# Two experts' layers whose results are folded into the layer that follows them, and their first product a block ahead

## The chip, the core and the metric

The program runs on one core of one Trainium2 chip. The metric is the device time of one execution in microseconds (us); three executions of the kernel before took 2326.70, 2327.89 and 2333.26 us, median 2327.89. The engines are TensorE (PE, with its weight loads PEld), VectorE (DVE), ScalarE (ACT), GpSimd (POOL) and SyncE (SP, which here only issues DMAs). Each works through its own queue of instructions in order and waits for the others by semaphores.

## The reference, cut to what matters

x is [4, 1024, 128] in f32: 4096 tokens of width 128. The program computes these layers one after the other, each with a layer norm ahead of it and a residual behind:

```python
x = x + moe(layernorm(x))        # 8 experts, top 2, capacity, hidden 512
x = x + mamba(layernorm(x))      # d_inner 256, 16 states, conv of 4
x = x + moe(layernorm(x))        # the same weights again
x = x + 0.5 * soft(layernorm(x)) # 64 experts x 32 slots: x -> slots -> experts -> x
x = x + gla(layernorm(x))        # gated linear attention
x = x + 0.5 * soft(layernorm(x))
```

For the mixture of experts the part that matters is its end: every token has two slots (first and second choice), each expert's output for a slot is stored, and

```python
gathered = out[idx_k, loc_c]                       # [tokens, 2, 128]
y = einsum('tk,tkd->td', gates_k * valid, gathered)
```

so a token's new x is x + gate0 * row0 + gate1 * row1. After that, each token is normed by itself (mean and variance over its 128 values).

## The kernel before, in words

x stays in SBUF the whole time as 32 tiles of 128 tokens x 128 values; the code counts tiles (j, g) and treats four as a group, so there are eight groups. Each layer norm has three small arrays of one or two values a tile: mv (mean and variance), rstd and nmr (minus mean times rstd). `ln_group` (L137) fills them for one group: four pairs of bn_stats and bn_aggr on DVE (L121, L122), eps added on DVE (L123), a power of minus one half on POOL (L130), nmr on DVE (L133). `ln_apply` (L142) then norms one tile with one activation on ACT (L143).

**Experts.** `moe_layer` (L148) routes the tokens (transposed tiles xT, L242, and stores of the normed rows to DRAM, xn_d, on ACT's DMA queue), then runs the experts over 16 blocks of four slot tiles of 128 slots. For a block, POOL gathers the four tiles' rows by indirect DMA (L346), PE turns them (L364) and DVE copies them out (dT, L366), PE makes the hidden layer in four products ph (L374) which ACT takes out with relu (hT, L378), PE makes the output po (L388), DVE adds the bias (eo, L393), and POOL scatters the four tiles by indirect DMA to y_d in DRAM (L352), to the place of their token and choice. The loop (L399 to L418) writes hidden(blk), then gathers three blocks ahead alternating with scatters of the block before, then turn(blk + 1), then output(blk). It stands in a hand-ordered region: every compute engine's queue keeps the order in which the code is written, and only SP's queue is placed by the scheduler.

**Combine.** When all blocks are scattered, the eight groups are brought back (L421 to L438): for a group, two loads of y (both choices) on SP (L425), four activations on ACT that multiply the first choice by its gate (L427), four scalar_tensor_tensors on DVE that multiply the second choice by its gate and add x (L431), one add on DVE that writes x (L435), and then `after(j)`, the `ln_group` of the next layer's norm.

**Mamba.** `mamba_layer` (L441) cuts the sequence into four halves (2 sequences x 2). Each half has a `prologue` (L490), a generator that yields after each small step: norm four tiles (xn), turn them (pt) and copy (xT, L502), the convolution and the input products pu (L521), activations, the projection, the store of B and C rows to DRAM (bc_d), and the softplus chain of ACT and DVE that ends in delta and du (L577 to L583). The first half's prologue runs alone ahead of the main loop (L706), the others are spread into the loop. The main loop has 64 units; per unit DVE scans and POOL multiplies (L620, L638, L654).

**Between.** `soft_weights` norms the slot vectors phi (phiT) and makes a bias row that is stored to DRAM (pb_d, L789) and read back into phiT's last row (L790). In front of the soft layer a second phi (phiM) is copied from it (L1580), a row of minus ones (mone) is written over its last row by a DMA (L1583), and the branch on a flag is taken.

**Soft layer.** `soft_bounded` (L813) has a first phase of 64 steps k (half a tile's logits each): PE makes the logits l (L870), DVE their row minimum (nmh, L874), ACT the exponential ex (L879), DVE the sums over 32 slots and their reciprocal (sm, L886, L887), POOL the product dm (L891), PE adds it into px (L902). All is written in one loop (L1053) whose order is kept on each engine. Before it the first four tiles are normed, turned and copied to xT (L861), which POOL first presets with ones (L836); smod (L807, L810) is a small constant. The norm of the next four tiles runs in the steps themselves. The second phase (clogits, cexpo, cweigh, mix, finish) uses phiM, and its large tiles L come from the pool lp.

Of the kernel before, what the change touches and what calls it, by code (L numbers as in the profile page):

```python
# [8 lines left out]
F32 = mybir.dt.float32  # L9
# [8 lines left out]
P = 128  # L18
# [50 lines left out]
def macaron_kernel(ctx: ExitStack, tc: tile.TileContext, a: dict, out: bass.AP):  # L69
# [48 lines left out]
    def ln_stats(ln, j0, n=4):  # L118
        for j in range(j0, j0 + n):
            st = small.tile([P, 6], F32, name="st", bufs=4)  # L120
            nc.vector.bn_stats(st, x[:, j, :])  # L121
            nc.vector.bn_aggr(ln[0][:, j, :], st)  # L122
        nc.vector.tensor_scalar(  # L123
            ln[1][:, j0 : j0 + n], ln[0][:, j0 : j0 + n, 1], EPS, None, ALU.add
        )

    def ln_root(ln, j0, n=4):
        mv, rstd, nmr = ln
        js = slice(j0, j0 + n)
        nc.gpsimd.tensor_tensor(  # L130
            rstd[:, js], rstd[:, js], half_t.to_broadcast([P, n]), ALU.pow
        )
        nc.vector.scalar_tensor_tensor(  # L133
            nmr[:, js], mv[:, js, 0], -1.0, rstd[:, js], ALU.mult, ALU.mult
        )

# [11 lines left out]
    def moe_layer(w1, w2, b2, tag, ln, after):  # L148

        xn_d = dram.tile([T, D], F32, name=f"xn_d{tag}")  # L150
        with ExitStack() as s:
# [3 lines left out]
            gate = rp.tile([P, K, NT], F32, name="gate")  # L155
# [178 lines left out]
            with ExitStack() as s1:  # L334
                gp = s1.enter_context(tc.tile_pool(name=f"gath{tag}", bufs=16))
                wk = s1.enter_context(tc.tile_pool(name=f"ework{tag}", bufs=2))
                yp = s1.enter_context(tc.tile_pool(name=f"ey{tag}", bufs=3))
                ps = s1.enter_context(tc.tile_pool(name=f"eps{tag}", bufs=2, space=PSUM))
                psh = s1.enter_context(tc.tile_pool(name=f"epsh{tag}", bufs=3, space=PSUM))
# [59 lines left out]
                AHEAD = 3  # L399
                with tc.manual_schedule(engines=ENGINES):  # L400
                    for c in range(AHEAD * 4):
                        gather(c)
                    turn(0)
                    for blk in range(NBLK + 1):
                        if blk < NBLK:
                            hidden(blk)
# [8 lines left out]
                        if blk + 1 < NBLK:  # L415
                            turn(blk + 1)
# [3 lines left out]

                y_v = y2_d[: K * T, :].rearrange("(k j p) d -> p k j d", k=K, p=P)  # L421
                for j in range(0, NT, 4):
                    y = yp.tile([P, K, 4, D], F32, name="y")
                    for k in range(K):
                        nc.sync.dma_start(out=y[:, k, :, :], in_=y_v[:, k, j : j + 4, :])  # L425
                    for i in range(4):
                        nc.scalar.activation(  # L427
                            y[:, 0, i, :], y[:, 0, i, :], AF.Copy,
                            scale=gate[:, 0, j + i : j + i + 1],
                        )  # L430
                        nc.vector.scalar_tensor_tensor(  # L431
                            y[:, 1, i, :], y[:, 1, i, :], gate[:, 1, j + i : j + i + 1],
                            x[:, j + i, :], ALU.mult, ALU.add,
                        )
                    nc.vector.tensor_tensor(  # L435
                        x[:, j : j + 4, :], y[:, 0, :, :], y[:, 1, :, :], ALU.add
                    )
                    after(j)  # L438


    def mamba_layer(ln, ln_next):  # L441
# [3 lines left out]
        with ExitStack() as s:  # L445
# [258 lines left out]
            with tc.manual_schedule(engines=ENGINES):  # L704

                for _ in prologue(*halves[0], rs[0], psa, "dA"):  # L706
                    pass
# [105 lines left out]
    def soft_bounded(phiN, phiM, pbc, ew, eb, tag, ln, after=None, last=False):  # L813
# [11 lines left out]
        with ExitStack() as s:  # L825
# [4 lines left out]
            lp = s.enter_context(tc.tile_pool(name=f"slp{tag}", bufs=15))  # L830
# [218 lines left out]
            with tc.manual_schedule(engines=ENGINES):  # L1049
                for i in range(4):  # L1050
                    norm(i)
                turn(0)
                take(0)  # L1053
                for k in range(NK + CS * NB + XL + 3):
                    if k < NK:
# [487 lines left out]
    def moe(tag, ln, after):  # L1543
# [120 lines left out]
```

## Time and profile before

| | us |
|---|---|
| median of three executions | 2327.89 |
| the profiled execution | 2379.35 |
| its span, first to last instruction | 2377.5 |
| experts of the first layer, 76 to 269 | PE busy 148.0, POOL 126.8 |
| its combine, 269 to 304 | PE 4.9, DVE 26.4 |
| Mamba's first half, 304 to 345 | PE 17.2, ACT 19.2, DVE 9.1 |
| Mamba's loop, 345 to 881 | |
| route of the second experts' layer, 881 to 954 | |
| its experts, 954 to 1146 | |
| its combine, 1146 to 1188 | PE 2.2, DVE 26.9 |
| soft layer, first phase, 1188 to 1410 | PE 216.5, DVE 165.5, ACT 83.1, POOL 114.7 |
| soft layer, second phase, 1410 to 1682 | |
| gated linear attention, 1682 to 1878 | |
| second soft layer, 1878 to 2377 | |

A row of the profile gives a start in us, a duration, the engine, the line of the kernel, the operation, what it writes and reads (partitions x elements), how many instructions were joined to the row, and in square brackets how long the engine stood idle before it and what ended that. Times of the stages are read off the trace at the first instruction that belongs to a stage; stages overlap a little on single engines. All durations come from the one profiled execution. The granted clock of TensorE was 0.908 of full over the span, 0.50 in the second combine and 0.99 in the first phase of the first soft layer.

### The profile page before, as it was taken

How to read it: one execution, taken by the hardware profiler on the slowest of the kernel's cores; microseconds unless marked ns; L12 is line 12 of the kernel's file. 1: busy time of each engine (PE TensorE's matmuls, PEld its weight loads, DVE VectorE, ACT ScalarE, POOL GpSimd, SP SyncE). 2: the span in 40 equal slices, each digit the busy share in tenths (PEclk: the TensorE clock that was granted, in tenths of full speed). 3: DMA queues.
4: the chain of work that ended last, by engine and by line, in shares of the span. 5: the costliest groups of instructions: out<-in, count | busy, mean ns of one | idle time of the engine just before them, and what ended most of it. 6: DMA issues, size and time to landing. Idle time of an engine off the chain costs nothing. (4 is left out here: it accounts for less than half of the span.)

```text
span 2377.5 us, 17972 instructions
## 1 busy us (share of the span) xinstructions
PE 1946.3 (82%) x5889; PEld 908.7 (38%) x5889; DVE 1406.0 (59%) x1947; ACT 925.7 (39%) x1453; POOL 1399.4 (59%) x896
## 2 busy tenths in 40 slices
PE   4677548888888864777299998999888799989998
PEld 3444312333333324445144444444232344434443
DVE  4311438888888965111477764666688677764444
ACT  3222346565555523122233334333344233333331
POOL 1666428888888871666345556665344355556663
PEclk9999869999989885799699999999888699999999
DMA  6111322333232333111200000000000000000000
GB/s 239 34 44 46 91 99 94 111 98 103 94 110 94 110 127 111 43 47 42 83 1 0 0 1 1 1 1 0 6 0 1 1 0 0 1 1 5 9 10 15
DMA packets 63677, 111.23 MB, mean 47 GB/s; under 512 B 7999, under 2 KB 41423, under 8 KB 58581
## 3 DMA queue, kind: packets, MB, share of 16 engines
q1 hardware_dynamic: 45062, 81.37, 10.4%
q0 software_dynamic: 8192, 16.79, 2.5%
q10 hardware_dynamic: 10322, 11.85, 1.5%
q8 instruction: 48, 0.79, 0.1%
q14 instruction: 53, 0.43, 0.1%
HBM read 90.53 MB, written 19.44 MB: 46 GB/s over the span
## 5 line engine op out<-in xcount | busy, mean ns | idle before, releaser
L891 POOL TENSOR_TENSOR dm<-ex,sm 128x1024 f32<-128x1024 f32 x128 | 244.6, 1912 | 219.3 <-DVE sm L887 125.5
L654 POOL TENSOR_TENSOR hc<-hst,Cs 128x1024 f32<-128x1024 f32 x128 | 290.1, 2277 | 70.9 <-DVE hst L638 66.5
L669 PE MATMUL py<-hc,ident 128*128 128x512 f32 x512 | 279.6, 679 | 39.4 <-POOL hc L654 39.3
L999 POOL TENSOR_TENSOR acc<-acc,L 128x1024 f32<-128x1024 f32 x96 | 225.8, 2352 | 114.5 <-ACT L L991 113.9
L991 ACT ACTIVATE L<-pl,pbc 128x512 f32<-128x512 f32 x256 | 161.9, 683 | 282.6 <-PE pl L981 278.2
L870 PE MATMUL l<-phiT,xT 128*128 128x512 f32 x512 | 247.1, 607 | 15.2 <-ACT xT L861 8.7
L879 ACT ACTIVATE ex<-l,nmh 128x1024 f32<-128x1024 f32 x128 | 142.7, 1115 | 286.4 <-DVE nmh L874 284.2
L981 PE MATMUL pl<-xT,phiM 128*128 128x512 f32 x512 | 242.8, 598 | 0.0
L1025 PE MATMUL py<-L,yt 128*128 128x512 f32 x512 | 238.4, 593 | 4.4 <-DVE L L1015 4.4
L902 PE MATMUL px<-dm,xn 128*128 128x512 f32 x512 | 240.8, 593 | 0.9 <-POOL dm L891 0.9
L874 DVE TENSOR_REDUCE nmh<-l 128x1 f32<-128x1024 f32 x128 | 156.5, 1222 | 108.8 <-PE l L870 108.8
L628 ACT ACTIVATE dA<-delta,A 128x512 f32<-128x512 f32 x256 | 179.2, 722 | 93.0 <-DVE hst L638 89.9
L374 PE MATMUL ph<-dT,w 128*128 128x512 f32 x256 | 145.5, 682 | 60.8 <-ACT hT L378 43.5
L620 POOL TENSOR_TENSOR dBu<-du,Bs 128x1024 f32<-128x1024 f32 x80 | 172.7, 2159 | 37.9 <-ACT dA L628 37.9
L378 ACT ACTIVATE hT<-ph,cols 128x512 f32<-128x512 f32 x128 | 84.6, 686 | 283.4 <-PE ph L374 176.9
L352 POOL DMA_INDIRECT y_d<-eo,dest x128 | 125.8, 983 | 91.4 <-DVE eo L393 60.8
L669 PEld LDWEIGHTS py<-hc,ident 128*128 128x128 f32 x512 | 97.9, 205 | 199.0 <-issue 121.8
L638 DVE TENSOR_TENSOR_SCAN hst<-dA,carry,dBu 128x512 f32<-128x512 f32 x128 | 154.1, 1258 | 5.6 <-POOL dBu L620 5.6
L886 DVE TENSOR_REDUCE sm<-ex 128x32 f32<-128x1024 f32 x128 | 154.6, 1208 | 0.0
L870 PEld LDWEIGHTS l<-phiT,xT 128*128 128x128 f32 x512 | 97.4, 193 | 146.6 <-issue 115.9
L638 DVE TENSOR_TENSOR_SCAN hst<-dA,dBu 128x512 f32<-128x512 f32 x128 | 146.5, 1199 | 7.6 <-POOL dBu L620 7.5
L1015 DVE TENSOR_TENSOR L<-L,rd 128x1024 f32<-128x1024 f32 x128 | 147.0, 1210 | 0.1
(248 smaller groups left out, 2866.3 us busy)
## 6 DMA issues: line engine op xcount, KB each, us to landing
Cs<-bc_d SPq DMA_DIRECT2D x32, 1024.0 KB, 4.7
Bs<-bc_d SPq DMA_DIRECT2D x80, 256.0 KB, 3.3
w<-in_w SPq DMA_DIRECT2D x4, 2048.0 KB
y<-y_d SPq DMA_DIRECT2D x32, 256.0 KB, 3.5
y_d<-zero SPq DMA_DIRECT2D x1, 4096.0 KB
ew<-in_ew ACTq DMA_DIRECT2D x1, 4096.0 KB
x<-in_x SPq DMA_DIRECT2D x8, 256.0 KB, 8.5
xn_da<-xn ACTq DMA_DIRECT2D x8, 256.0 KB, 14.7
```

Source lines behind the costliest of these rows:

```text
L620: eng.tensor_tensor(dBu, r["du"], r.pop(("B", n)).unsqueeze(2).to_broadcast([P, HB, NC]), ALU.mult,)
L628: nc.scalar.activation(dA, r["delta"][:, :, c], AF.Exp, scale=A[:, c * DS + n : c * DS + n + 1],)
L638: nc.vector.tensor_tensor_scan(hst[:, :, c], r.pop(("dA", n, c)), dBu[:, :, c], 0.0 if h == 0 else carry[b][:, c, n : n + 1], ALU.mult, AL ...
L654: nc.gpsimd.tensor_tensor(hc, r.pop(("h", n)), Cs.unsqueeze(2).to_broadcast([P, HB, NC]), ALU.mult)
L669: nc.tensor.matmul(r["py"][:, c, :], ident, hc[:, :, c], start=False, stop=(n == DS - 1))
L870: nc.tensor.matmul(l[:, q * 512 : (q + 1) * 512], xT[:, j * P : (j + 1) * P], phiN[:, o : o + 512], start=True, stop=True,)
L891: nc.gpsimd.tensor_tensor(dms[k], exs.pop(k), sms.pop(k).unsqueeze(2).to_broadcast([P, NG, PS]), ALU.mult,)
L902: nc.tensor.matmul(px[hf * 2 + q], xns[j // 4][:, j % 4, :], dmf[:, q * 512 : (q + 1) * 512], start=(j == 0), stop=(j == NT - 1),)
L981: nc.tensor.matmul(pl[:, i, :], phiM[:, (2 * c + i) * P : (2 * c + i + 1) * P], xT[:, t * TB : (t + 1) * TB], start=True, stop=True,)
L991: nc.scalar.activation(L[:, i, :], pl[:, i, :], AF.Exp, bias=pbc[:, 2 * c + i : 2 * c + i + 1], scale=-1.0,)
L999: nc.gpsimd.tensor_tensor(accs[t], accs[t], L, ALU.add)
L1025: nc.tensor.matmul(pys[t], yt[:, 2 * c + i, :], L[:, i, :], start=(c + i == 0), stop=(c == CS - 1 and i == 1),)
```

## The change

- `moe_layer` ends with the last scatter. The combine becomes a function of its own, which returns `bring(j)` (the two loads of a group) and `pieces(j)`, a generator that does a group in eight pieces: four activations and two scalar_tensor_tensors; the other two; the add; two pairs of norm sums; two pairs and eps; POOL's power; the load of a later group; nmr. The gates move to tiles that live as long as the program.
- Mamba brings four groups, runs all pieces of group 0, and then runs three pieces after each yield of the first half's prologue. What is left runs behind it.
- The soft layer, inside the branch, brings two groups, runs group 0, norms and turns the first block, runs group 1, and then runs one piece ahead of each step k of its loop: groups 2 to 7 in steps 0 to 47. Only the first soft layer does this.
- The copy phiM, mone and its DMA are written ahead of the second experts' layer instead of inside the branch.
- The experts: hidden(blk + 1) and turn(blk + 2) are written where hidden(blk) and turn(blk + 1) were, with turn(1) and hidden(0) ahead of the loop, four blocks gathered ahead for three, 20 gather buffers for 16, three work buffers for two, four PSUM buffers of ph for three.
- The pool lp has 14 buffers for 15.

```diff
@@ -115,24 +115,37 @@
             const.tile([P, NT], F32, name=f"nmr{tag}"),
         )
-    def ln_stats(ln, j0, n=4):
+    def ln_sums(ln, j0, n=4):
         for j in range(j0, j0 + n):
             st = small.tile([P, 6], F32, name="st", bufs=4)
             nc.vector.bn_stats(st, x[:, j, :])
             nc.vector.bn_aggr(ln[0][:, j, :], st)
+    def ln_eps(ln, j0, n=4):
         nc.vector.tensor_scalar(
             ln[1][:, j0 : j0 + n], ln[0][:, j0 : j0 + n, 1], EPS, None, ALU.add
         )
-    def ln_root(ln, j0, n=4):
...
+    def ln_pow(ln, j0, n=4):
+        js = slice(j0, j0 + n)
+        nc.gpsimd.tensor_tensor(
+            ln[1][:, js], ln[1][:, js], half_t.to_broadcast([P, n]), ALU.pow
+        )
+    def ln_minus(ln, j0, n=4):
         mv, rstd, nmr = ln
         js = slice(j0, j0 + n)
-        nc.gpsimd.tensor_tensor(
-            rstd[:, js], rstd[:, js], half_t.to_broadcast([P, n]), ALU.pow
-        )
         nc.vector.scalar_tensor_tensor(
             nmr[:, js], mv[:, js, 0], -1.0, rstd[:, js], ALU.mult, ALU.mult
         )
+    def ln_root(ln, j0, n=4):
+        ln_pow(ln, j0, n)
+        ln_minus(ln, j0, n)
     def ln_group(ln, j0):
         ln_stats(ln, j0)
@@ -145,14 +158,13 @@
         )
-    def moe_layer(w1, w2, b2, tag, ln, after):
+    def moe_layer(w1, w2, b2, tag, ln, gate):
         xn_d = dram.tile([T, D], F32, name=f"xn_d{tag}")
         with ExitStack() as s:
             rp = s.enter_context(tc.tile_pool(name=f"route{tag}", bufs=1))
             src = rp.tile([P, NSB], I32, name="src")
             dest = rp.tile([P, NSB], I32, name="dest")
-            gate = rp.tile([P, K, NT], F32, name="gate")
             with ExitStack() as s1:
                 tp = s1.enter_context(tc.tile_pool(name=f"rtmp{tag}", bufs=1))
@@ -332,11 +344,10 @@
             with ExitStack() as s1:
-                gp = s1.enter_context(tc.tile_pool(name=f"gath{tag}", bufs=16))
-                wk = s1.enter_context(tc.tile_pool(name=f"ework{tag}", bufs=2))
-                yp = s1.enter_context(tc.tile_pool(name=f"ey{tag}", bufs=3))
+                gp = s1.enter_context(tc.tile_pool(name=f"gath{tag}", bufs=20))
+                wk = s1.enter_context(tc.tile_pool(name=f"ework{tag}", bufs=3))
                 ps = s1.enter_context(tc.tile_pool(name=f"eps{tag}", bufs=2, space=PSUM))
-                psh = s1.enter_context(tc.tile_pool(name=f"epsh{tag}", bufs=3, space=PSUM))
+                psh = s1.enter_context(tc.tile_pool(name=f"epsh{tag}", bufs=4, space=PSUM))
                 NBLK = NSB // 4
                 gs, dTs, hTs, eos = {}, {}, {}, {}
                 spacer = wk.tile([P, 1], F32, name="spacer")
@@ -396,14 +407,18 @@
-                AHEAD = 3
+                AHEAD = 4
                 with tc.manual_schedule(engines=ENGINES):
                     for c in range(AHEAD * 4):
                         gather(c)
                     turn(0)
+                    turn(1)
+                    hidden(0)
                     for blk in range(NBLK + 1):
-                        if blk < NBLK:
-                            hidden(blk)
+                        if blk + 2 < NBLK:
+                            turn(blk + 2)
+                        if blk + 1 < NBLK:
+                            hidden(blk + 1)
                         for i in range(4):
                             c = (blk + AHEAD) * 4 + i
                             if c < NSB:
@@ -412,33 +427,66 @@
                                 nc.gpsimd.memset(spacer, 0.0)
                             if blk > 0:
                                 scatter((blk - 1) * 4 + i)
-                        if blk + 1 < NBLK:
-                            turn(blk + 1)
                         if blk < NBLK:
                             output(blk)
-                y_v = y2_d[: K * T, :].rearrange("(k j p) d -> p k j d", k=K, p=P)
-                for j in range(0, NT, 4):
-                    y = yp.tile([P, K, 4, D], F32, name="y")
-                    for k in range(K):
-                        nc.sync.dma_start(out=y[:, k, :, :], in_=y_v[:, k, j : j + 4, :])
-                    for i in range(4):
-                        nc.scalar.activation(
-                            y[:, 0, i, :], y[:, 0, i, :], AF.Copy,
-                            scale=gate[:, 0, j + i : j + i + 1],
-                        )
-                        nc.vector.scalar_tensor_tensor(
-                            y[:, 1, i, :], y[:, 1, i, :], gate[:, 1, j + i : j + i + 1],
-                            x[:, j + i, :], ALU.mult, ALU.add,
-                        )
-                    nc.vector.tensor_tensor(
-                        x[:, j : j + 4, :], y[:, 0, :, :], y[:, 1, :, :], ALU.add
-                    )
-                    after(j)
-    def mamba_layer(ln, ln_next):
+    def combine(yp, gate, ln, n=2):
+        y_v = y2_d[: K * T, :].rearrange("(k j p) d -> p k j d", k=K, p=P)
+        ys = {}
+        def bring(j):
+            if j < NT:
+                y = ys[j] = yp.tile([P, K, 4, D], F32, name="y")
+                for k in range(K):
+                    nc.sync.dma_start(out=y[:, k, :, :], in_=y_v[:, k, j : j + 4, :])
+        def second(j, i):
+            nc.vector.scalar_tensor_tensor(
+                ys[j][:, 1, i, :], ys[j][:, 1, i, :], gate[:, 1, j + i : j + i + 1],
+                x[:, j + i, :], ALU.mult, ALU.add,
+            )
+        def pieces(j):
+            y = ys[j]
+            for i in range(4):
+                nc.scalar.activation(
+                    y[:, 0, i, :], y[:, 0, i, :], AF.Copy,
+                    scale=gate[:, 0, j + i : j + i + 1],
+                )
+            second(j, 0)
+            second(j, 1)
+            yield
+            second(j, 2)
+            second(j, 3)
+            yield
+            nc.vector.tensor_tensor(
+                x[:, j : j + 4, :], y[:, 0, :, :], y[:, 1, :, :], ALU.add
+            )
+            yield
+            ln_sums(ln, j, 2)
+            yield
+            ln_sums(ln, j + 2, 2)
+            ln_eps(ln, j)
+            yield
+            ln_pow(ln, j)
+            yield
+            del ys[j]
+            bring(j + 4 * n)
+            yield
+            ln_minus(ln, j)
+            yield
+        return bring, pieces
+    def run(pieces):
+        for _ in pieces:
+            pass
+    def mamba_layer(ln, ln_next, first):
         HB = 512
         NJ = HB // P
         bc_d = dram.tile([B, 2, 2, DS, HB], F32, name="bc_d")
@@ -702,9 +750,17 @@
                     f(rs[units[k][0]], units[k][1])
             with tc.manual_schedule(engines=ENGINES):
+                bring, pieces = first
+                for j in range(0, 16, 4):
+                    bring(j)
+                run(pieces(0))
+                others = (_ for j in range(4, NT, 4) for _ in pieces(j))
                 for _ in prologue(*halves[0], rs[0], psa, "dA"):
-                    pass
+                    for _ in range(3):
+                        next(others, None)
+                run(others)
                 for k in range(3):
                     at(fetch, k)
                 at(feed, 0)
@@ -827,7 +883,7 @@
             xnp = s.enter_context(tc.tile_pool(name=f"sxn{tag}", bufs=3))
             ep = s.enter_context(tc.tile_pool(name=f"sep{tag}", bufs=3))
             dp = s.enter_context(tc.tile_pool(name=f"sdp{tag}", bufs=4))
-            lp = s.enter_context(tc.tile_pool(name=f"slp{tag}", bufs=15))
+            lp = s.enter_context(tc.tile_pool(name=f"slp{tag}", bufs=14))
             wk = s.enter_context(tc.tile_pool(name=f"swk{tag}", bufs=4))
             psl = s.enter_context(tc.tile_pool(name=f"spl{tag}", bufs=2, space=PSUM))
             psm = s.enter_context(tc.tile_pool(name=f"spm{tag}", bufs=4, space=PSUM))
@@ -1047,11 +1103,21 @@
             SEAM = 3
             WL, XL = 10, 12
             with tc.manual_schedule(engines=ENGINES):
+                if first:
+                    bring, pieces = first
+                    bring(0)
+                    bring(4)
+                    run(pieces(0))
                 for i in range(4):
                     norm(i)
                 turn(0)
                 take(0)
+                others = iter(())
+                if first:
+                    run(pieces(4))
+                    others = (_ for j in range(8, NT, 4) for _ in pieces(j))
                 for k in range(NK + CS * NB + XL + 3):
+                    next(others, None)
                     if k < NK:
                         logits(k)
                         expo(k)
@@ -1549,45 +1615,61 @@
             nc.sync.dma_start(
                 out=b2.rearrange("p e d -> p (e d)"), in_=a["b2"].partition_broadcast(P)
             )
-            moe_layer(w1, w2, b2, tag, ln, after)
+            moe_layer(w1, w2, b2, tag, ln, gate)
     lns = [ln_begin(i) for i in range(6)]
+    gates = [const.tile([P, K, NT], F32, name=f"gate{i}") for i in range(2)]
     for j in range(0, NT, 4):
         ln_group(lns[0], j)
-    moe("a", lns[0], lambda j: ln_group(lns[1], j))
+    moe("a", lns[0], gates[0])
     spool = ctx.enter_context(tc.tile_pool(name="softw", bufs=1, side="right"))
     phiN, pbc, flag = soft_weights(spool)
-    mamba_layer(lns[1], lns[2])
+    with tc.tile_pool(name="ya", bufs=4) as yp:
+        mamba_layer(lns[1], lns[2], combine(yp, gates[0], lns[1], 4))
     spool2 = ctx.enter_context(tc.tile_pool(name="softw2", bufs=1, side="right"))
     ew, eb = expert_weights(spool2)
+    phiM = spool2.tile([D, NS], F32, name="phiM")
+    nc.scalar.copy(phiM, phiN)
+    mone = spool2.tile([1, 512], F32, name="mone")
+    nc.vector.memset(mone, -1.0)
+    nc.sync.dma_start(
+        out=phiM[D - 1 : D, :].rearrange("o (r c) -> o r c", c=512),
+        in_=mone.unsqueeze(1).to_broadcast([1, NS // 512, 512]),
+    )
     for j in range(0, NT, 16):
         ln_root(lns[2], j, 16)
-    moe("b", lns[2], lambda j: ln_group(lns[3], j))
-    def rest(soft):
-        soft("a", lns[3], lambda j: ln_group(lns[4], j))
+    moe("b", lns[2], gates[1])
+    def behind_soft(soft):
         gla_layer(lns[4], lns[5])
         for j in range(0, NT, 16):
             ln_root(lns[5], j, 16)
         soft("b", lns[5], last=True)
+    def after(j):
+        ln_group(lns[4], j)
     bounded = nc.values_load(flag, min_val=0, max_val=1)
     with tc.If(bounded > 0) as cmp:
-        with tc.tile_pool(name="softm", bufs=1) as pool:
-            phiM = pool.tile([D, NS], F32, name="phiM")
-            nc.scalar.copy(phiM, phiN)
-            mone = pool.tile([1, 512], F32, name="mone")
-            nc.vector.memset(mone, -1.0)
-            nc.sync.dma_start(
-                out=phiM[D - 1 : D, :].rearrange("o (r c) -> o r c", c=512),
-                in_=mone.unsqueeze(1).to_broadcast([1, NS // 512, 512]),
-            )
-            rest(lambda *a_, **k: soft_bounded(phiN, phiM, pbc, ew, eb, *a_, **k))
+        def soft(*a_, **k_):
+            soft_bounded(phiN, phiM, pbc, ew, eb, *a_, **k_)
+        with tc.tile_pool(name="yb", bufs=2) as yp:
+            soft("a", lns[3], combine(yp, gates[1], lns[3]), after)
+        behind_soft(soft)
     with cmp.Else():
+        def soft(*a_, **k_):
+            soft_layer(phiN, ew, eb, *a_, **k_)
         nc.scalar.activation(phiN, phiN, AF.Copy, scale=-1.0)
-        rest(lambda *a_, **k: soft_layer(phiN, ew, eb, *a_, **k))
...
```

More of the change, by code (lines that the diff above doesn't have):

```diff
@@ L125, in ln_stats @@
         )
-    def ln_root(ln, j0, n=4):
+    def ln_stats(ln, j0, n=4):
+        ln_sums(ln, j0, n)
+        ln_eps(ln, j0, n)
+    def ln_pow(ln, j0, n=4):
[4 more added lines that the diff above has]
+    def ln_minus(ln, j0, n=4):
         mv, rstd, nmr = ln
         js = slice(j0, j0 + n)
-        nc.gpsimd.tensor_tensor(
-            rstd[:, js], rstd[:, js], half_t.to_broadcast([P, n]), ALU.pow
-        )
         nc.vector.scalar_tensor_tensor(
@@ L811, in group_sum, with soft_bounded @@
         return smod
-    def soft_bounded(phiN, phiM, pbc, ew, eb, tag, ln, after=None, last=False):
+    def soft_bounded(phiN, phiM, pbc, ew, eb, tag, ln, first=None, after=None, last=False):
         TB = 512
@@ L1540, in gla_layer, with moe @@
                     next(behind, None)
-    def moe(tag, ln, after):
+    def moe(tag, ln, gate):
         with ExitStack() as s:
@@ L1574, in rest @@
         soft("b", lns[5], last=True)
+    def after(j):
+        ln_group(lns[4], j)
     bounded = nc.values_load(flag, min_val=0, max_val=1)
     with tc.If(bounded > 0) as cmp:
-        with tc.tile_pool(name="softm", bufs=1) as pool:
-            phiM = pool.tile([D, NS], F32, name="phiM")
-            nc.scalar.copy(phiM, phiN)
-            mone = pool.tile([1, 512], F32, name="mone")
-            nc.vector.memset(mone, -1.0)
-            nc.sync.dma_start(
-                out=phiM[D - 1 : D, :].rearrange("o (r c) -> o r c", c=512),
-                in_=mone.unsqueeze(1).to_broadcast([1, NS // 512, 512]),
-            )
-            rest(lambda *a_, **k: soft_bounded(phiN, phiM, pbc, ew, eb, *a_, **k))
+        def soft(*a_, **k_):
[3 more added lines that the diff above has]
+        behind_soft(soft)
     with cmp.Else():
+        def soft(*a_, **k_):
+            soft_layer(phiN, ew, eb, *a_, **k_)
         nc.scalar.activation(phiN, phiN, AF.Copy, scale=-1.0)
-        rest(lambda *a_, **k: soft_layer(phiN, ew, eb, *a_, **k))
+        with tc.tile_pool(name="yc", bufs=2) as yp:
+            bring, pieces = combine(yp, gates[1], lns[3])
+            bring(0)
+            bring(4)
+            for j in range(0, NT, 4):
+                run(pieces(j))
+        soft("a", lns[3], after=after)
+        behind_soft(soft)
 def kernel(**inputs):
```

## The prediction, made before the changed kernel was run

> **What bounds the kernel now.** I read the windows by stage first, then the timeline at each seam that the edit touches, then the groups of the lines it moves. The two combine stages (the experts' rows read back, added to x, normed) stand almost alone: from 269 to 304 us PE is busy 4.9 of 35 us, from 1146 to 1188 us 2.2 of 42. The first half of Mamba, 304 to 345, has PE 17, ACT 19, DVE 9 of 41 us: nothing full. The soft layer's first phase, 1188 to 1410, is the opposite: PE 216.5 of 222 us, DVE 165.5, POOL 114.7. So work may be laid into the prologue for little, into the soft loop only where DVE and POOL let it.
>
> The seams in the timeline (start, duration, engine, line, operation, idle before it and what ended that):
>
> ```profile
> 269.51 3.62 SPq L425 DMA_DIRECT2D y<-y_d  x6
> 272.45 1.28 ACT L427 ACTIVATE y<-y,gate 128x128 f32<-128x128 f32 x4 [1.49 <-DMA y<-y_d]
> ...
> 303.21 1.65 ACT L143 ACTIVATE xn<-x,nmr,rstd 128x128 f32<-128x128 f32 x4 [6.06 <-issue]
> ...
> 312.12 8.76 PE L521 MATMUL pu<-xT,cw 128*128 128x512 f32 x16 [5.39 <-DVE cw L466]
> ...
> 1146.88 23.32 SPq L425 DMA_DIRECT2D y<-y_d  x16
> ...
> 1183.16 3.51 POOL L836 MEMSET xT<- 32x4096 f32 x1
> ...
> 1187.34 8.23 PE L870 MATMUL l<-phiT,xT 128*128 128x512 f32 x12 [6.22 <-ACT xT L861]
> ```
>
> Between the first load of y and the first useful step of the next layer lie 33.7 us in the first seam (xn, 303.21) and 40.5 in the second (logits, 1187.34). One step of the soft loop, 3.44 us by its repeats:
>
> ```profile
> 1217.47 1.22 DVE L874 TENSOR_REDUCE nmh<-l 128x1 f32<-128x1024 f32 x1 [0.70 <-PE l L870]
> 1218.62 1.21 DVE L886 TENSOR_REDUCE sm<-ex 128x32 f32<-128x1024 f32 x1
> ...
> 1219.86 0.35 DVE L887 RECIPROCAL sm<-sm 128x32 f32<-128x32 f32 x1
> 1220.36 1.91 POOL L891 TENSOR_TENSOR dm<-ex,sm 128x1024 f32<-128x1024 f32 x1 [1.53 <-ACT xn L143]
> ```
>
> DVE's three rows end to end take 2.74 us (1217.47 to 1220.21), which leaves 0.70 free a step. PE is the bound, DVE is close behind.
>
> The median to start from is 2327.9 (three runs, 2326.7 to 2333.3). The profiled execution took 2379.4 (span 2377.5), 51.5 more. Its experts stages explain that: POOL needs 8 issues of 1.28 us (0.97 to 0.99 plus 0.30) a block of work, 163.5 us for 128, so from the first gather at 76.5 it would end at 240.0; it ended at 268.0, because PE's completions are held about 6 us every second block. That is 27.7 a layer and 55 for two, so I take those stalls as belonging to the recording. Changes are worked out on the profile and subtracted from the median.
>
> **Mamba's seam.** Removed from ahead of the prologue: seven of eight groups (four activations, four scalar_tensor_tensors, add, norm sums, pow, nmr). Group 0 stays. On SP's queue the y loads now stand behind the write of pb_d (274.01) and the read of phi's extra row, which before came after them; the nearest write-then-read on one queue here (bc_d 329.97, Bs 331.63) takes 1.6, so the first y load goes at about 276.1 in place of 269.5, 6.6 later. First activation 2.9 after that, 279.1; group 0 alone takes 6.0 (0.85 until the adders start, 1.14 for four, 0.69 add, 1.66 for four norm pairs, 0.17, 1.18 pow, 0.26): xn at 285.1, **18.1 earlier**. pu started 8.9 after xn behind late weights; they load early now, so 4.9, **+4.0**. Given back inside the prologue: two groups' activations on ACT, which carries the chain there (2 x 1.28), and the tail after the last yield (activations and add 2.0, norm sums 1.8, a pow waiting for DVE 1.0, nmr 0.2), together **-7.6**. Net **+14.5**; 22 if the loads don't stand behind pb_d, 8 if each of seven groups costs its 1.28 on ACT.
>
> **Soft layer's seam.** Group 0 goes as above, group 1 behind norm and turn of the first block. xT's memset and smod's copy (to 1186.7 before) now run while the last scatter lands. First logits 11.7 us after the first y load instead of 40.5: 28.7. The first nmh waits for group 1's pieces and two adders of group 2 on DVE: -2.2. So **+26.5** before the loop pays.
>
> In the loop the pieces bring DVE, per group of eight steps, 4 x 0.34 + 0.69 + 1.66 + 0.17 + 0.16 = 4.1 us, 0.5 a step against 0.70 free. By durations alone this is hidden by PE's 3.44. But here a rule speaks against the change. The rows first:
>
> ```profile
> 340.86 1.23 DVE L580 TENSOR_TENSOR l<-l,w 128x1024 f32<-128x1024 f32 x1
> ...
> 393.83 3.10 POOL L654 TENSOR_TENSOR hc<-hst,Cs 128x1024 f32<-128x1024 f32 x1
> ...
> 394.99 3.02 DVE L580 TENSOR_TENSOR l<-l,w 128x1024 f32<-128x1024 f32 x1
> ...
> 1505.97 2.34 POOL L999 TENSOR_TENSOR acc<-acc,L 128x1024 f32<-128x1024 f32 x1
> 1506.04 2.30 DVE L133 SCALAR_TENSOR_TENSOR nmr<-mv,rstd 128x4 f32<-128x4 f32 x1 [1.13 <-POOL rstd L130]
> ```
>
> The same add takes 1.23 alone and 3.02 begun inside a POOL operation; four elements, 0.16 alone, took 2.30, to the end of POOL's. But L1015, with one operand in PSUM, keeps 1.21 beside POOL's adds. The Trainium skill ("SBUF — State Buffer", section "SBUF: two separate sides") says why: VectorE and GpSimd share a port pair under an exclusive lock, and a VectorE operation with two SBUF inputs waits out the whole GpSimd operation. The moved adders (y and x), the add (y and y) and nmr (mv and rstd) have two SBUF inputs; POOL's dm holds the pair 1.91 of every 3.44 us and starts just as DVE comes free. The eps row L123, one input, was also held once (0.79 at 439.89). By durations alone the loop costs 0; by the rule, laid out step by step with dm where it stands: two steps of adders 5.27 and 5.24 (the first slips in, the second waits 1.9), add 3.40, sums 3.55, sums and eps 4.97, then 2.74, 2.74 and 2.95 of DVE work. Those are 30.9 against 27.5, the long steps not being made up by the short: +3.4 a group. Five groups (the second's lies in the start) give 17, less 2.5 of slack in the two logits buffers: **-14.5**. I take the rule's value, since the rows agree on it. Bounds: 0, and 46 if every step with such an operation loses a full dm (rival E). Net of the seam **+12**.
>
> **Route b.** phiM's copy (1.88, ACT idle then), its memset and a store-and-load move ahead of the second route. ACT's stores of xn take rotating completion slots in turn; phiM's DMA takes one, so the first store waits for w1 where it waited for ew, the second for w2:
>
> ```profile
> 893.43 0.58 ACT L242 COPY xT<-pt 128x512 f32<-128x512 f32 x1 [9.67 <-DMA ew<-in_ew]
> ```
>
> One group more stands behind w2 (906.9), and one free-running group is 3.29 (912.35 to 915.63): **-3.3**; 0 if the slots fall otherwise.
>
> **Experts.** hidden a block earlier, turn two earlier, four blocks gathered ahead, more buffers. In the recording eo's period is 23.8 us per two blocks, POOL's floor 20.5. Unrecorded I take them as bound by POOL's queue, whose 128 issues stay: **0**. Bounds: +10 to +25 if PE's held completions are partly there without recording too; -2 for four more gathers ahead of the first scatter and the longer fill. Gates in a longer-lived pool and lp 14 instead of 15: 0, no wait for an lp buffer is near that depth; without it one step, 3.4.
>
> **Sum:** 14.5 + 12 - 3.3 + 0 = 23.2; 2327.9 - 23.2 = **2304.7**, say 2305 (recorded, 2356).
>
> **Rivals.**
> A, as worked out: 2305, own range 2297 to 2313. Chance 0.47.
> B, the lock costs nothing: DVE's adders fall into the 1.5 us between two dm's, since the whole loop shifts with PE. For: dm leaves that gap each step. Against: dm is released by the same reciprocal after which the adders stand. 14.5 + 26.5 - 3.3 = 37.7: 2290. Chance 0.22.
> C, the experts gain unrecorded too, 10 to 25: with A's rest 2288. For: 60.8 us of POOL's idle time before its scatters ended with eo. Against: POOL's floor fits the unrecorded time within 4 us. Chance 0.08.
> D, Mamba's net at its low end and the loop near 25: 8 + 1.5 - 3.3 = 6, within 0.3% of before. Chance 0.12.
> E, slower: in the soft loop all five steps of a group with a two-input operation or eps wait a whole dm: 5 x 1.91 = 9.6, of which the 1.5 us that eight steps' free 5.6 leave over 4.1 are taken up: 8.1 a group. As ACT and POOL slip too, the second group pays as well: six groups, 48.6 - 2.5 = 46. Then 37.7 - 46 = -8: 2336. For: POOL's acc caught nmr whole in every row like the one above. Against: an adder that comes first pays nothing. It decides from (37.7 + 2.5)/6 = 6.7 us a group. Chance 0.11.
>
> **How the numbers follow.** 0.3% of 2328 is 7 us, about what a measurement of this kernel can tell from no change. Faster: A, B, C = 0.77. Within 7 us: D and a third of E = 0.16. Slower: the rest of E, 0.07. The range goes from B's 2290 less 8 for an expert gain on top, 2282, to D's near side, 2322; it leaves out half of D, E and a corner of B with C, 0.2.
>
> **What would show it.** In the profile after: y's first load behind phi's row on SP; xn some 18 us nearer to the last scatter; the adders in the soft loop with rows of about 2.2 us beside dm (ten or more), eps over 1 us, and the steps 3.44 wherever no piece stands; the first phase of soft a longer by about 14; route b's xT waiting for w and not for ew; eo still at 23.8 per two blocks. I am wrong if adders keep 0.34 in the loop (B), if nearly all moved rows there are near 2 us and the phase grows by over 40 (E), if the experts' stage shrinks by 10 or more (C), or if the prologue grows by more than 15 us.

## The result, and the profile after

The changed kernel takes **2298.2 us** (median of four, 2293.8 to 2299.4) beside 2329.3 of the kernel before; the ratio is 0.9864, 95% interval 0.9845 to 0.9883, so 27 to 36 us faster. The forecast was 2305, 23 us faster, with a range of 2282 to 2322. Its own recording spans 2297.1 us.

On some chips the kernel before takes about 2386 us and on others about 2327, recorded or not, with some 56 of the 59 us in its two experts' stages (191 us each against 164), so each time below is compared with before's on the same chip, and the recording of before (2379), which has the long stages, with other recordings only outside these two.

Lengths of the stages in us. A scatter or gather counts by its issue on GpSimd: from the start of the first gather's, to the end of the last scatter's.

| | before | after |
|---|---|---|
| experts, first layer: first gather to last scatter | 191.5 | 164.4 |
| last scatter to Mamba's first scan | 78.0 | 64.4 |
| Mamba's loop: first to last scan | 525.2 | 529.6 |
| second route: last scan to first gather | 82.9 | 85.5 |
| experts, second layer | 191.3 | 163.2 |
| last scatter to the first row minimum of soft a | 45.7 | 18.8 |
| row minima of soft a, first to last | 224.6 | 232.5 |
| everything behind | 961.7 | 963.0 |

The seams in the timeline of the kernel after, in the columns used before (start, duration, engine, line, operation, idle before it):

```profile
249.47 0.28 SPq L846 DMA_DIRECT2D phiT<-pb_d  x1
249.96 13.82 SPq L443 DMA_DIRECT2D y<-y_d  x12
...
253.06 1.28 ACT L454 ACTIVATE y<-y,gate 128x128 f32<-128x128 f32 x4 [5.07 <-DMA y<-y_d]
...
259.29 1.65 ACT L156 ACTIVATE xn<-x,nmr,rstd 128x128 f32<-128x128 f32 x4 [4.96 <-DVE nmr L142]
...
263.84 2.90 PE L569 MATMUL pu<-xT,cw 128*128 128x512 f32 x3 [2.38 <-issue]
...
1084.26 14.70 SPq L443 DMA_DIRECT2D y<-y_d  x8
...
1096.26 6.59 PE L926 MATMUL l<-phiT,xT 128*128 128x512 f32 x8 [0.77 <-ACT xT L917]
```

The issues of the last scatters end at 240.12 and 1082.87. In the first seam y's first load does stand behind phi's row on SP's queue, 9.8 us after the scatter; in the second it goes after 1.4. From the load to xn it is now 9.3 us for 33.7, to the first logits 12.0 for 40.5.

Two steps of the soft loop after, from the same timeline. The first carries a pair of adders (L446), the second the fifth piece (two pairs of sums and eps, L125):

```profile
1128.38 0.35 DVE L943 RECIPROCAL sm<-sm 128x32 f32<-128x32 f32 x1
1128.65 0.52 DVE L446 SCALAR_TENSOR_TENSOR y<-y,gate,x 128x128 f32<-128x128 f32 x2
1128.88 2.06 POOL L947 TENSOR_TENSOR dm<-ex,sm 128x1024 f32<-128x1024 f32 x1 [1.52 <-DVE sm L943]
1129.43 1.23 DVE L930 TENSOR_REDUCE nmh<-l 128x1 f32<-128x1024 f32 x1 [0.26 <-PE l L926]
...
1142.11 0.35 DVE L943 RECIPROCAL sm<-sm 128x32 f32<-128x32 f32 x1
...
1142.61 1.92 POOL L947 TENSOR_TENSOR dm<-ex,sm 128x1024 f32<-128x1024 f32 x1 [1.52 <-DVE st L121]
...
1143.05 0.18 DVE L122 BATCH_NORM_AGGREGATE mv<-st 128x2 f32<-128x6 f32 x1
1143.27 1.28 DVE L125 TENSOR_SCALAR rstd<-mv 128x4 f32<-128x4 f32 x1
1144.46 1.21 DVE L930 TENSOR_REDUCE nmh<-l 128x1 f32<-128x1024 f32 x1
```

The adders start 0.27 us after the reciprocal does, dm 0.50 after: they are in first, and POOL pays (2.06 for 1.91). The row minimum still waits for PE. eps comes in the middle of dm, takes 1.28 for 0.17, and the row minimum behind it is late. From one row minimum to the next it is 3.43 us in the steps with adders, add or nmr of the five later groups, and 4.74 in every fifth step of a group. (A step of 4.50 in every eight stands in the kernel before as well.)

The route, ACT's turned tiles (their idle time is ended by what they wait for):

```profile
860.71 0.59 ACT L254 COPY xT<-pt 128x512 f32<-128x512 f32 x1 [14.09 <-DMA w<-in_w]
869.70 0.59 ACT L254 COPY xT<-pt 128x512 f32<-128x512 f32 x1 [6.86 <-DMA w<-in_w]
872.98 0.59 ACT L254 COPY xT<-pt 128x512 f32<-128x512 f32 x1 [1.15 <-PE pt L251]
```

The first waits for w where it waited for ew in the kernel before.

### The profile page after: what moved, and what is told of

The parts are those of the page before. It is cut to its first block, busy times and chain, and to the rows that moved or that the text cites. A ratio compares the mean times of both kernels' runs of the same rounds, so it can differ in the third digit from the quotient of the medians.

```text
span 2297.1 us, 17954 instructions
## 1 busy us (share of the span) xinstructions
PE 1931.9 (84%) x5889; PEld 903.0 (39%) x5889; DVE 1418.5 (62%) x1947; ACT 928.1 (40%) x1453; POOL 1400.0 (61%) x904
## 5 line engine op out<-in xcount | busy, mean ns | idle before, releaser
L404 DVE TENSOR_TENSOR eo<-po,b 128x512 f32<-128x512 f32 x32 | 22.1, 692 | 207.4 <-PE po L399 207.4
```

## The experiments

Four kernels each take one part of the change alone, on a chip on which the kernel before takes 2387.0 (median of 37).

**The experts' order and buffers alone.**

```diff
-                AHEAD = 3
+                AHEAD = 4
...
+                    turn(1)
+                    hidden(0)
                     for blk in range(NBLK + 1):
-                        if blk < NBLK:
-                            hidden(blk)
+                        if blk + 2 < NBLK:
+                            turn(blk + 2)
+                        if blk + 1 < NBLK:
+                            hidden(blk + 1)
```

> The kernel before with the new order and buffers of the experts alone. Forecast's theory (unrecorded, POOL's issues bound both): within 3 us of before; in the recording the eo period may still be 23.8 us per two blocks. Rival (the new order removes PE's late completions): the recording has 20.5 per two blocks and a span about 55 us shorter than before's recording, and the unrecorded time is 5 to 6 us shorter, which is what is left of the 31 when the other stages' 25.6 (read from the two recordings) is taken off.

Measured: 2379.9, ratio 0.9971 (0.9960 to 0.9981), 7 us faster. Its recording has stages of 189.2 and 193.2 us, not 164: the new order does not remove the late completions of TensorE's products, and it is not the recording that makes them, since the unrecorded runs of before are as long. Neither theory fits. Where the 7 us lie is not shown: the two stages add up to 382.5 us here, and to 382.8 and 383.1 in the two recordings of the kernel before. What ended the idle time ahead of eo on DVE, and in the third row ahead of its scatters on POOL (us in all, times), where "remote" means that the profile shows no instruction which ended the wait:

```profile
  remote: 108.5, 7
  PE ph L374: 63.5, 6
  DVE eo L393: 60.5, 20
```

**The Mamba fold alone** (experts, soft layer and phiM as before; lp keeps 14 buffers).

```diff
-    moe("a", lns[0], lambda j: ln_group(lns[1], j))
+    moe("a", lns[0], gates[0])
...
-    mamba_layer(lns[1], lns[2])
+    with tc.tile_pool(name="ya", bufs=4) as yp:
+        mamba_layer(lns[1], lns[2], combine(yp, gates[0], lns[1], 4))
```

> The kernel before with the first layer's results folded into Mamba's first half alone. By the recordings of before and after: 13.6 us gained from the last scatter to the first scan and 4.4 given back in Mamba's loop, so 9 us faster. If the 4.4 in the loop is a chance of phase between VectorE and GpSimd and not of the fold, the loop's length (scan to scan 525.2 before, 529.6 after) comes out elsewhere, and the gain is 13.6 minus another number.

Measured: 2371.5, ratio 0.9932 (0.9909 to 0.9955), 16 us faster. Last scatter to first scan is 64.1 us, 14.0 less than before, and the loop 526.3. By the recording the fold gains 14.0 and the loop loses 1.2, which lies within the 11 to 22 us of the interval; the loop's length is taken up below.

**The soft fold alone** (lp with 14 buffers here too).

```diff
-    moe("b", lns[2], lambda j: ln_group(lns[3], j))
+    moe("b", lns[2], gates[1])
...
+        with tc.tile_pool(name="yb", bufs=2) as yp:
+            soft("a", lns[3], combine(yp, gates[1], lns[3]), after)
```

> The kernel before with the second layer's results folded into the soft layer's loop alone. By the recordings: 26.9 gained up to the first row minimum, 7.9 given back in the loop (six groups of 1.3), so 19 us faster. The forecast's lock estimate would leave 12; no lock at all 26.5.

Measured: 2370.2, ratio 0.9930 (0.9904 to 0.9956), 17 us faster. To the first row minimum 18.9 us (26.9 gained), the row minima 234.2 (9.6 given back): 17.3. The 1.7 beyond the changed kernel's 7.9 lie in the soft loop's fifth and sixth intervals, where the granted clock was 0.70 and 0.50 in two stretches of 2 us (1184 to 1188) and 1.00 in the changed kernel; the run with the old order of the experts below has the same dip and the same 234.2.

**phiM ahead of the second experts' layer alone.**

```diff
     ew, eb = expert_weights(spool2)
+    phiM = spool2.tile([D, NS], F32, name="phiM")
+    nc.scalar.copy(phiM, phiN)
...
+    nc.sync.dma_start(out=phiM[D - 1 : D, :]...)
...
-            lp = s.enter_context(tc.tile_pool(name=f"slp{tag}", bufs=15))
+            lp = s.enter_context(tc.tile_pool(name=f"slp{tag}", bufs=14))
```

> The kernel before with phiM's copy, its row and its DMA ahead of the second experts' layer alone (and 14 buffers in lp). Completion-slot theory: the route's turned tiles wait for w instead of ew, the stage from Mamba's last scan to the second layer's first gather grows from 82.9 to 85.5, so 2.6 us slower. If nothing hangs on the slot: 0; the copy itself is hidden, so up to 2 us may also be won ahead of the soft layer.

Measured: 2389.8, ratio 1.0006 (0.9992 to 1.0021): between 2 us won and 5 lost, not resolved by the times. In its recording the route is 86.3 us for 82.9, and the first turned tile waits for w. Over all recordings the route takes 81.5 to 83.7 us where phiM's row is not ahead of it on SP's queue, and 85.5 to 87.3 where it is:

```profile
904.97 0.58 ACT L242 COPY xT<-pt 128x512 f32<-128x512 f32 x1 [14.69 <-DMA w<-in_w]
914.12 0.58 ACT L242 COPY xT<-pt 128x512 f32<-128x512 f32 x1 [7.02 <-DMA w<-in_w]
917.40 0.58 ACT L242 COPY xT<-pt 128x512 f32<-128x512 f32 x1 [1.16 <-PE pt L239]
```

The following, but for the last, are on chips on which before takes 2326 to 2328.

**The changed kernel again.**

> The changed kernel again, beside the kernel before on one chip. If late PE completions in the experts' stages belong to the chip and not to the recording, then on a chip where before's median is near 2387 this kernel too shows experts' stages of about 190 us each instead of 164, and comes out near 2387 - 25.6 - 7 (the experts' order alone gave 7 there) = 2354; on a chip where before is near 2328 it is 2298 again.

Measured: 2299.7, ratio 0.9874 (0.9849 to 0.9899), experts' stages 164.4 and 163.2. Mamba's loop took 532.5 us in this recording and 529.6 in the first, of one and the same program.

**The changed kernel with the old order of the experts** (the first diff the other way).

> The changed kernel with the experts' order and buffers of before. Forecast (POOL's issues bound both orders): equal to the changed kernel within 3 us, experts' stages of 164. Rival (each order's period is PE's chain, too): on a chip where before is near 2328 the stages are 2 to 3 us longer each, so 5 to 6 us slower than the changed kernel, near 2304; on a chip where before is near 2387, 7 us.

Measured: 2297.4, ratio 0.9870 (0.9855 to 0.9885), stages 163.8 and 163.4: equal. POOL's 128 issues of 1.28 are 163.5, so on these chips either order is at POOL's floor, and the experts' part of the change is worth nothing. Here all of DVE's waits before eo were ended by PE's product, and "remote" does not occur:

```profile
  PE po L399: 115.8, 32
```

**eps at the head of the sixth piece.**

```diff
             ln_sums(ln, j + 2, 2)
-            ln_eps(ln, j)
             yield
+            ln_eps(ln, j)
             ln_pow(ln, j)
```

> The changed kernel with eps moved from the end of the fifth piece to the head of the sixth. Reading of the trace: only eps meets dm in the loop (1.28 us and a row minimum 1.3 us late, six times in all), because it is the one operation that comes long after the reciprocal. Then the first phase loses only what is left of the 7.9: about 6.5 to 7.5 us faster than the changed kernel on the same chip, and the steps 12, 20, 28, 36, 44 are back at 3.43. If the two-input operations as such are the cost, as the forecast had it, nothing changes.

Measured: 2293.0, 6.7 below the changed kernel's median on that chip. The ratios to before, 0.9846 (0.9823 to 0.9868) and 0.9874 (0.9849 to 0.9899), overlap, but the recordings settle it: the row minima take 224.7 us here and in the two later kernels with this edit, as before the change (224.6), against 232.5 in the changed kernel both times, and all five steps are 3.43. Behind the reciprocal eps takes 0.11:

```profile
1146.15 0.35 DVE L943 RECIPROCAL sm<-sm 128x32 f32<-128x32 f32 x1
1146.42 0.11 DVE L125 TENSOR_SCALAR rstd<-mv 128x4 f32<-128x4 f32 x1
1148.27 1.22 DVE L930 TENSOR_REDUCE nmh<-l 128x1 f32<-128x1024 f32 x1 [1.75 <-PE l L926]
```

So one badly placed instruction of four elements was the whole loss in the loop, and the six groups' adders, adds and nmr cost nothing that shows.

**Each piece behind the row minimum.**

```diff
-                    next(others, None)
                     if k < NK:
                         logits(k)
+                        next(others, None)
                         expo(k)
```

> The changed kernel with each piece written behind the row minimum of its step instead of ahead of it. The adders then start while dm holds the shared port: each first adder should take 1 us or more instead of 0.25, the exponential is not held (it waits for the row minimum alone) but the sums and reciprocal behind are, so dm and the next steps slip. By the forecast's lock estimate 3.4 us a group, 20 in all, slower than the changed kernel's 1.3 a group: about 12 us slower than it. If the place does not matter, 0.

Measured: 2297.5, 2 below the changed kernel, within the noise; row minima 230.6 us, 6.0 over before. A miss in size and sign: VectorE is held here, as these rows show (two adders in 1.33 for 0.52, the add in 1.61 for 0.69), but the row minimum runs beside dm for 1.2 of its 1.9 us and the waits are short:

```profile
1131.56 1.22 DVE L930 TENSOR_REDUCE nmh<-l 128x1 f32<-128x1024 f32 x1
1132.70 1.33 DVE L446 SCALAR_TENSOR_TENSOR y<-y,gate,x 128x128 f32<-128x128 f32 x2
...
1136.55 1.61 DVE L464 TENSOR_TENSOR x<-y 128x512 f32<-128x512 f32 x1
```

The step with the second pair of adders takes 3.91 us and the one with the add 4.12, while eps, here behind dm, is free again: about 1.0 a group against 1.3.

**phi's preparation ahead of the first layer.**

```diff
-    moe("a", lns[0], gates[0])
     spool = ctx.enter_context(tc.tile_pool(name="softw", bufs=1, side="right"))
     phiN, pbc, flag = soft_weights(spool)
+    moe("a", lns[0], gates[0])
```

> The changed kernel with the preparation of phi written ahead of the first experts' layer, so that y's first load does not stand behind phi's row on SyncE's queue (9.8 us after the last scatter; 1.4 in the second layer). The load should go some 8 us earlier. If the load is what the first activation waits for, 5 to 8 us faster than the changed kernel, less what phi's 16 products and loads cost the first route, which is not full of PE work (0 to 3).

Measured: 2292.7, ratio 0.9847 (0.9830 to 0.9864), 7.0 below the changed kernel. y's load goes 1.3 us after the last scatter, and the first scan comes 55.7 us after it for 64.4: the whole 8.7. The first route pays for it: its first gather is at 79.5, where the recordings without this edit have it at 75.4 to 77.5.

**Three edits together, phi's row on GpSimd's queue.** eps as above, and

```diff
-            nc.sync.dma_start(out=pb_d.rearrange(...), in_=pb)
-            nc.sync.dma_start(out=phiN[D - 1 : D, :], in_=pb_d)
+            nc.gpsimd.dma_start(out=pb_d.rearrange(...), in_=pb)
+            nc.gpsimd.dma_start(out=phiN[D - 1 : D, :], in_=pb_d)
...
-    nc.sync.dma_start(out=phiM[D - 1 : D, :]...)
+    nc.gpsimd.dma_start(out=phiM[D - 1 : D, :]...)
```

> The changed kernel with eps at the head of the sixth piece, phi's row (store and load) on GpSimd's queue and phiM's row on GpSimd's queue. Parts: eps 7.8 (shown); y's first load 8 us earlier, but phi's own work keeps ScalarE and VectorE until 8 us after the last scatter, so only 4 to 5 of it; phiM's row off SyncE's completion slots, so the route from Mamba's last scan to the second first gather back from 85.5 to 82.9, 2.6. Sum 14 to 15: near 2285 beside a 2300 of the changed kernel. If the slot is not the cause of the route's 2.6, 12.

Measured: 2287.8, ratio 0.9829 (0.9815 to 0.9842), by the ratios 8 to 10 below the changed kernel, where 14 to 15 were expected. eps gave its 7.8 and the route 1.9 (83.6 us; its first turned tile waits for ew again), but the load of y gave nothing: it went at 251.62, 11.4 us after the scatter, and the first scan came 65.6 us after it for 64.4. SP's load of the branch's flag, which depends on phi too, had come to stand ahead of it:

```profile
L842 DVE TENSOR_SCALAR flag<-nm x1: 134/134/134, 250.3 to 250.3; 1x1 int32<-1x1 f32 x1
L1654 SPq TENSOR_LOAD <-flag x1: 473/473/473, 250.4 to 250.4; - x1
```

In the changed kernel that load was at 258.4, behind the first loads of y. A wait taken off a queue that the scheduler orders let in the next one.

**Three edits together, phi ahead of the first layer.** eps and phiM's queue as above, phi as in the run before that.

> As the kernel before in this list, but with phi's preparation ahead of the first experts' layer instead of on another queue (8.7 gained from last scatter to first scan, 3.8 lost in the first route, as the earlier run showed). Parts: eps 7.8, phi 5, phiM's row 2.6: 15, near 2285. Mamba's loop, whose length moved between 525 and 532 with no change in its code, may add or take 4.

Measured: **2282.5**, ratio 0.9808 (0.9794 to 0.9821): 44 us below before, and by the ratios 13 to 15 below the changed kernel. Last scatter to first scan 55.7, second route 83.1, row minima 224.7.

**The kernel before, recorded again.**

> The kernel before, unchanged, recorded once more beside itself. If the late PE completions (experts' stages of 191 us each in its first recording) belong to the chip, then on a chip where it takes about 2328 us the recording shows stages of 164 and a span of 2324 to 2330, and on one where it takes 2387 stages of 191 again. If Mamba's loop length is chance and not the change's, its scan to scan comes out anywhere from 525 to 532; if it is the change's, at 525 again.

Measured: 2385.0 on a chip on which before takes 2386.5; stages of 191.5 and 191.6. Mamba's loop took 529.9 us, where the first recording of this same kernel had 525.2. So its length moves by 5 us with nothing changed. The rows that differ most are of one operation on DVE, here in the timeline of this recording and then in the first one, both 47 us after the first scan:

```profile
393.14 8.02 DVE L579 SCALAR_TENSOR_TENSOR w<-w,e 128x1024 f32<-128x1024 f32 x1
401.20 1.23 DVE L580 TENSOR_TENSOR l<-l,w 128x1024 f32<-128x1024 f32 x1
```

```profile
393.21 1.74 DVE L579 SCALAR_TENSOR_TENSOR w<-w,e 128x1024 f32<-128x1024 f32 x1
```

It takes 1.23 alone. In the changed kernel it was 8.01 too, from 351.06 to 359.07:

```profile
349.57 2.16 POOL L668 TENSOR_TENSOR dBu<-du,Bs 128x1024 f32<-128x1024 f32 x1
351.66 4.23 POOL L702 TENSOR_TENSOR hc<-hst,Cs 128x1024 f32<-128x1024 f32 x2
355.82 2.16 POOL L668 TENSOR_TENSOR dBu<-du,Bs 128x1024 f32<-128x1024 f32 x1
```

It began inside the first of these and waited through all four operations, which follow without a gap to 357.98. In the second recording of the changed kernel there was another one of 6.98. This operation is not the whole of it, though: behind it the scans are 2.6 us later in this recording than in the first and soon after only 0.9, and the rest of the 4.8 comes in later places. The loop took 527.0 us in the run with the old order, which has such a row of 8.03, and 528.4 to 528.8 in three runs without any. Over all recordings it is 525.2 to 530.3 us in five with before's way into Mamba (mean 527.3) and 526.3 to 532.5 in nine with the fold (mean 529.0). By the means some 2 us could be the fold's, which is less than the spread; one recording against one can't tell.

## Why the prediction was right, and where it was wrong

The sum with measured terms: 13.6 (Mamba's seam) + 26.9 (soft seam) - 7.9 (loop) - 2.6 (route) + 0 (experts) = **30.0**, beside 31.1 measured and 23.2 forecast. The 4.4 in Mamba's loop is left out, as mostly chance (about 1.7 by the means of all recordings). Of the 6.8 by which the forecast fell short of this sum, 6.6 lie in one term. The mechanism of both seams held; the lock's share in the soft loop did not, and what came of it lay nearer to rival B: the adders keep 0.34, which the prediction had named as a sign of being wrong. With eps's cost gone the time is 2293.0, outside A's own 2297 to 2313: that the changed kernel lies within it is partly luck.

- **Mamba's seam**, forecast 14.5, measured 13.6 (14.0 with this part alone). xn is 16.0 nearer to the scatter, forecast 18.1: y's load lost 8.4 behind phi's row and not 6.6, because phi's last product ends 6.4 us after the last scatter's issue, for 4.2 before, and the store of its row goes at 7.9 for 6.0. pu gained 4.4 (forecast 4.0). Inside the prologue and behind it 6.7 went back (forecast 7.6). The queue that the load was moved past was the right thing to count: with phi out of the way 8.7 come back. (The upper bound of 22 is 21 by the prediction's own terms, 14.5 and 6.6.)
- **Soft seam**, forecast 26.5 up to the first row minimum, measured 26.9.
- **The lock**, forecast 14.5, measured 7.9: the term that was mis-sized. It failed at "two steps of adders 5.27 and 5.24 (the first slips in, the second waits 1.9)". Both adders slip in, 0.17 apart, since dm starts 0.23 later than they do, and it is dm that waits, by 0.15. Those two steps measured 3.43. "sums and eps 4.97" was right at 4.74, and is all that there is: five groups of 1.30, and 1.4 for the group whose pieces lie in the first steps, which the forecast counted as free. The rule that was weighed (an exclusive port pair, VectorE's operation waiting out GpSimd's) fits the rows of after as those of before; what was left out of the layout was the other side, that an operation which comes first does not wait. The prediction had this as the argument against rival E, and allowed it to the first adder alone. With eps moved B's size of the loop comes out (224.7 for 224.6), though not by B's way: the adders do not fall between two dm's, they stand ahead of one.
- **The route**, forecast 3.3, measured 2.6 in the changed kernel and 3.4 alone: first waits as described. That the slot is the cause stands on the recordings (w for ew with the DMA there, ew again and 1.9 to 2.4 us back when it goes by GpSimd's queue); the times of that part alone don't resolve it.
- **Experts**, forecast 0 because POOL's issues bound them: right on the chips where before takes about 2327, since taking the order back changes nothing there. But the ground given, "I take those stalls as belonging to the recording", was wrong, as unrecorded times near 2386 show, so that the zero held is partly luck: the changed kernel was timed on chips without the stalls. "eo still at 23.8 per two blocks" failed accordingly (20.5, POOL's floor). On a chip with the stalls the order was worth 7, so rival C has a grain of truth there, though no recording shows in which stage.

## What to carry to other kernels

Small operations laid into a loop beside a GpSimd operation are free or dear by their place: right behind the instruction that releases GpSimd they are in first, a microsecond later even four elements wait. When work is moved past a queue, list what the queue still holds after the mend too, since the next item may hang on the same late result. And before a gap between a recording and a median is explained by the recording, see whether both are from one chip. A stage's length out of one recording is a sample: compare it with every recording in which that stage is the same.

## What the hardware showed that was not expected

Late completions of TensorE's products in the experts' stages came on some chips and not on others: 189 to 196 us a stage in six recordings, 163 to 165 in the other eight, with either order of the products. The granted clock does not tell them apart: the second stage of the last recording above had 0.90 and took 191.6 us, that of the changed kernel 0.90 and 163.2; the first stage had 0.89 and 189.2 us in the run of the experts alone, 0.89 and 164.4 with phi ahead of the first layer. In the six, 7 to 12 waits before VectorE's add end by "remote" and make up 72 to 109 us, 9 to 15 each on average; in the eight there are none. Every one of these ended with TensorE's semaphore, which moved 1.5 to 8.9 us after the last of TensorE's instructions on record had ended. The same six recordings hold only 1443 to 1512 updates of the semaphores that tell of the gathers' and scatters' landing, where the changed kernel's hold 4096, so the delay could lie in how such updates arrive and not in TensorE; that is not shown. What holds the completions was not found: no run here took a possible cause away, and as each chip was used at one time only, chip and time can't be told apart.

An operation on VectorE can lose to GpSimd several times over. One begun 0.6 us before the end of GpSimd's either goes next (1.74 us in all, and GpSimd's next takes 3.10 for 2.13) or waits for three more (8.0). Which of the two comes out differs between executions of one program.
